# The experts' tokens gathered in 128-feature pieces and turned by VectorE, in an attention-and-experts kernel

## The chip, the core and the metric

The kernel runs on one core of a Trainium2 chip. Time is the device time of the program in microseconds (us); where several executions were timed, their median. A profile is one further execution with the profiler on; its span is the time from its first to its last instruction.

The engines: TensorE (PE in the profile; PEld is its weight loads), VectorE (DVE), ScalarE (ACT), GpSimd (POOL), which also issues the indirect DMAs, and SyncE (SP), which issues most of the others. Each engine runs its own instructions in order.

## The reference, cut to what matters

The input is x, 8 sequences of 256 tokens with 512 features. A first layer adds a gated long convolution (heads of width 8, a causal filter per head) of ctx with the normalised x to x. The second layer, in which most of the change lies, is a mixture of 16 experts; each token goes to 4 of them, each expert takes at most 256 tokens, and a shared expert works on all:

```python
scores = softmax(x @ gate_w.T); topk_w, topk_i = top_k(scores, 4)
topk_w = topk_w / (topk_w.sum(-1) + 1e-20)
# buf: the tokens of each expert by rank, at most CAP = 256; wbuf: their weights
xg = xpad[buf]
mid = silu(einsum('ech,ehi->eci', xg, w_gate)) * einsum('ech,ehi->eci', xg, w_up)
eout = einsum('eci,eih->ech', mid, w_down) * wbuf[..., None]
y = zeros.at[buf].add(eout)
shared = silu(x @ sw_gate) * (x @ sw_up) @ sw_down
```

Here x is the layer-normalised token, h runs over 512 features and i over 352 hidden units. The kernel returns x plus both.

## The kernel before, in words

All arithmetic that counts is in fp32. A tile is 128 tokens (16 of them, in the order row, then batch); 512 features are NC = 4 chunks of 128. The program order of every engine is the order of the source lines; waits come from the data only.

**Attention part** (a loop over 16 tiles n, L690). Each turn convolves two heads' worth of rows on TensorE (attend, L443, L457) with elementwise work on VectorE and GpSimd. Between these stand steps for neighbouring tiles. The new tokens of tile n-1 are normalised (xn, L745) and stored by store() (L535) to xw_d, a table in DRAM with one row per token: 512 features and 16 expert weights (ROW = 528 elements). For ten of the tiles (MILD, n = 3 to 12) the token-to-feature transpose, xnT, which the router and the shared expert use, isn't made on TensorE. ScalarE writes the normalised tile once more, with its columns permuted (xp, L749), four DMAs send it to a DRAM scratch (send_blocks, L376), one fetches it with 32-token blocks in place (fetch_blocks, L386), and VectorE transposes 32 by 32 blocks (transpose_blocks, L391, L393). The keys and queries of the next tile go the same way (kp, qp). The other tiles are transposed on TensorE (transpose_in, L126) and copied out by ScalarE. masks() (L190) makes small constant tables, in three steps in turns 6, 7 and 8.

**Shared expert.** shared_block() (L131) is a generator; fill(k) runs k steps of it wherever it stands, so that TensorE has work while others prepare. What is left runs in the loop at L921.

**Routing.** For expert e, compare(e) (L859) marks in hot which token has which slot; find(e) (L870) turns that by 16 bf16 matmuls (L875) and five small VectorE operations (L883 to L891) into idx[:, e, n], the row number for each of the 256 slots (two halves n of 128). Empty slots point to zero rows behind the tokens.

**Experts** (a loop over e, L1031; one turn is called a slot below). The order in the source is the order on each engine:
- gate_up(e): 16 matmuls with 128x256 operands for two full hidden blocks (L970; the profile counts two records for each) and the rest of 96 columns in a packed form (L982, L990); SiLU on ScalarE, products into mid on VectorE (L978, L1000, L1004)
- tokens(e+1) (L938): the gathered rows of the next expert, transposed by TensorE, 8 times 128x128 (L128), and copied out by ScalarE (L942) into xgT
- find(e+2) and gather(e+2) (L925): two indirect DMAs of GpSimd (L929), each 128 rows of 2112 bytes from xw_d, weights included
- down(e, n) for both halves: 6 matmul records each (L1012), a scaling by the slot's weight on VectorE (L1020; the weight is column 512 + e of the gathered row), and an indirect DMA of GpSimd that adds the rows to out (L1021). Each such scatter waits until the one before it has landed, since both add to the same array
- compare(e+3), and the weight loads of expert e+2 by SyncE (L816 to L821)

Gathers for experts 0 and 1 are issued ahead of the loop (L1029), and the first tokens(0) there too (L1030). The weights of the slots are written into xw_d by 16 DMAs at L915.

Chunk c holds features 128c to 128c+127, in xgT as in the rows of the weights (L816, L817: partition p of chunk c is row 128c + p).

Of the kernel before, what the change touches and what calls it, by code (L numbers as in the profile page):

```python
# [20 lines left out]
P = 128  # L21
BK = 32
# [10 lines left out]
ROW = L + E  # L33
# [19 lines left out]
def ssm_attention__then__moe_kernel(  # L53
# [34 lines left out]
    xw_d = dram.tile([T + CAP, ROW], F32, name="xw_d")  # L88
# [35 lines left out]
    def transpose_in(src):  # L124

        pt = ps_tr.tile([P, NC, P], F32, name="pt")  # L126
        for c in range(NC):
            nc.tensor.transpose(pt[:, c, :], src[:, c * P : (c + 1) * P], ident)  # L128
        return pt

# [59 lines left out]
    def masks():  # L190
# [27 lines left out]
        nc.gpsimd.tensor_copy(empty, empty_i)  # L218
        yield
# [13 lines left out]
        nc.vector.tensor_copy(tok, tok_f)  # L233
        yield
# [9 lines left out]
        masked.update(tri=tri, tri_b=tri_b, same_b=same_b, slot_f=slot_f, tok=tok, empty=empty)  # L244
        yield
# [3 lines left out]
    with ExitStack() as att:  # L249
# [284 lines left out]

        def store(n, xn):  # L535
            nc.sync.dma_start(out=by_tile(xw_d[0:T, 0:L])[n], in_=xn)
# [73 lines left out]
        for c in range(NC):  # L610
            rows = slice(c * P, (c + 1) * P)
            shared_pieces.append((swg[:, c, :], sw_gate[rows, 0 : NF * P]))
            shared_pieces.append((swu[:, c, :], sw_up[rows, 0 : NF * P]))
        rest = slice(NF * P, IS)
        by_chunk = lambda w: w[:, rest].rearrange("(c p) f -> p c f", p=P)
# [73 lines left out]
        sent_k = sent_q = sent_x = got_x = None  # L689
        for n in range(NT):  # L690
# [4 lines left out]
            tps = [toeps.pop(t * HT + hh) for hh in range(HT)]  # L695
            if more and n:
                for hh in range(HT):
                    load_blocks(seq[n + 1] * HT + hh)
            for i in range(2 if n == 0 else n + 3, min(n + 4, NT)):
                loaded[i] = load_tile(i)  # L700
            if swift and more:
                got_k, got_q = fetch_blocks(sent_k), fetch_blocks(sent_q)
# [5 lines left out]
            if n - 2 in MILD:  # L708
                transpose_blocks(xnT[:, :, n - 2, :], got_x)
# [28 lines left out]
            if n == 0:  # L738
                pg = ps_tr.tile([P, NC, P], F32, name="pg", tag="pt")
                for c in range(NC):  # L740
                    nc.tensor.transpose(pg[:, c, 0:E], gw[:, c * P : (c + 1) * P], ident[:E, :E])
                nc.scalar.copy(gwT[:, :, 0:E], pg[:, :, 0:E])
            fill(2)
            if n > 0:
                normalise(xn, xs[:, seq[n - 1], :], *xstats)  # L745
                store(seq[n - 1], xn)
                if n - 1 in MILD:
                    xp, by_block = in_blocks("xp")
                    normalise(by_block, chunked(xs[:, n - 1, :]), *xstats)  # L749
                    sent_x = send_blocks(xp)  # L750
# [14 lines left out]
            if n - 1 in MILD:  # L765
                got_x = fetch_blocks(sent_x)
            elif n > 0:
                nc.scalar.copy(xnT[:, :, seq[n - 1], :], transpose_in(xn))
                fill(1)
                ready(n - 1)  # L770
# [19 lines left out]
        nc.scalar.copy(xnT[:, :, NT - 1, :], transpose_in(xn))  # L790
# [7 lines left out]
        zeros = load.tile([P, ROW], F32, name="zeros", bufs=1)  # L798
        nc.gpsimd.memset(zeros, 0.0)
        for n in range(NSL):  # L800
            dst = slice(T + n * P, T + (n + 1) * P)
            nc.sync.dma_start(out=xw_d[dst, :], in_=zeros)
            nc.sync.dma_start(out=out[dst, :], in_=zeros[:, 0:L])
# [8 lines left out]
    def load_expert(e):  # L812
        w = wpool.tile([P, 2, NC, I], F32, name="w")
        wd = wpool.tile([P, NI, L], F32, name="wd")
        full = I // P * P
        nc.sync.dma_start(out=w[:, 0], in_=w_gate[e].rearrange("(c p) f -> p c f", p=P))  # L816
        nc.sync.dma_start(out=w[:, 1], in_=w_up[e].rearrange("(c p) f -> p c f", p=P))  # L817
        nc.sync.dma_start(
            out=wd[:, 0 : I // P, :], in_=w_down[e, 0:full, :].rearrange("(c p) f -> p c f", p=P)
        )  # L820
        nc.sync.dma_start(out=wd[0 : I - full, I // P, :], in_=w_down[e, full:, :])  # L821
        return w, wd
# [27 lines left out]
    for n in range(NSL):  # L850
        fill(1)
        nc.vector.tensor_mul(
            what[:, :, :, n, :],
            part[:, n].unsqueeze(3).broadcast_to([P, NT, E, 3]),
            tok.unsqueeze(2).broadcast_to([P, NT, E, 3]),
        )
    idx = route.tile([P, E, NSL], I32, name="idx")

# [11 lines left out]
    def find(e, hot):  # L870


        ip = ps_sm.tile([P, NSL, 3], F32, name="ip", tag="sm")
        for i in range(NT):
            nc.tensor.matmul(  # L875
                ip.rearrange("p n k -> p (n k)"),
                lhsT=hot[:, i, :],
                rhs=what[:, i, e].rearrange("p n k -> p (n k)"),
                start=(i == 0),
                stop=(i == NT - 1),  # L880
            )
        info = route.tile([P, NSL, 3], F32, name="info", bufs=2)
        nc.vector.tensor_copy(info, ip)  # L883
        who = route.tile([P, NSL], F32, name="who", bufs=2)
        gap = route.tile([P, NSL], F32, name="gap", bufs=2)
        nc.vector.scalar_tensor_tensor(
            who, info[:, :, 0], float(S), info[:, :, 1], ALU.mult, ALU.add
        )
        nc.vector.tensor_mul(gap, info[:, :, 2], empty)
        nc.vector.tensor_sub(gap, empty, gap)  # L890
        nc.vector.tensor_add(idx[:, e, :], who, gap)  # L891

# [10 lines left out]
    find(0, hots.pop(0))  # L903
    fill(2)
    nc.vector.tensor_reduce(tot, prob, AX.X, ALU.add)
# [8 lines left out]
    for n in range(NT):  # L914
        nc.sync.dma_start(out=by_tile(xw_d[0:T, L:ROW])[n], in_=prob[:, n, :])  # L915
# [3 lines left out]
    find(1, hots.pop(1))  # L919
    hots[2] = compare(2)  # L920
    while behind:  # L921
        fill(1)


    def gather(e):  # L925
        gs = []
        for n in range(NSL):
            g = ffn.tile([P, ROW], F32, name="g", bufs=6)
            nc.gpsimd.indirect_dma_start(  # L929
                out=g,  # L930
                out_offset=None,
                in_=xw_d[:, :],
                in_offset=bass.IndirectOffsetOnAxis(ap=idx[:, e, n : n + 1], axis=0),
            )
            gs.append(g)
        return gs

    def tokens(gs):  # L938

        xgT = ffn.tile([P, NC, CAP], F32, name="xgT")  # L940
        for n in range(NSL):
            nc.scalar.copy(xgT[:, :, n * P : (n + 1) * P], transpose_in(gs[n]))  # L942
# [65 lines left out]
    def down(e, n, mid, wd, g):  # L1008
# [11 lines left out]
        nc.vector.tensor_scalar_mul(o, po, g[:, L + e : L + e + 1])  # L1020
# [8 lines left out]
    gathered = {e: gather(e) for e in range(2)}  # L1029
    xgT_next = tokens(gathered[0])  # L1030
    for e in range(E):  # L1031
        w, wd = experts.pop(e)
        wt = pack(w)
        gs = gathered.pop(e)
        xgT = xgT_next
        mid = ffn.tile([P, NI, CAP], F32, name="mid")
        if e + 1 < E:
            gate_up(xgT, mid, w, wt, slice(0, CAP))
            xgT_next = tokens(gathered[e + 1])
            if e + 2 < E:  # L1040
                find(e + 2, hots.pop(e + 2))
                gathered[e + 2] = gather(e + 2)
            for n in range(NSL):
                down(e, n, mid, wd, gs[n])
            if e + 3 < E:
                hots[e + 3] = compare(e + 3)
        else:
# [3 lines left out]
            down(e, 0, mid, wd, gs[0])  # L1051
            gate_up(xgT, mid, w, wt, slice(P, CAP), range(1, NI))
            down(e, 1, mid, wd, gs[1])
# [40 lines left out]
```

## Time and profile before

| | us |
|---|---|
| median of 3 timed runs | 700.24 (698.79 to 700.52) |
| the profiled execution | 697.82 |
| its span | 696.1 |
| granted TensorE clock, mean | 0.994 |
| attention part, about | 0 to 342 |
| rest of the shared expert, with routing | 342 to 424 |
| experts 0 to 15 | 424 to 696 |

The costliest groups by line that the change touches or that stand beside it, from the profile's table of groups (busy time, mean of one):

| line, what | count | busy us | mean ns |
|---|---|---|---|
| L970 PE gate and up, 128x256 | 480 | 106.2 | 379 |
| L1012 PE down, 128x512 | 128 | 61.3 | 601 |
| L128 PE transposes of gathered rows | 128 | 16.6 | 273 |
| L942 ACT copy of them | 32 | 16.9 | 578 |
| L929 POOL gather | 32 | 32.0 | 1001 |
| L1021 POOL scatter | 32 | 51.0 | 1595 |
| L1020 DVE scaling | 32 | 24.0 | 751 |
| L393 DVE block transpose, 128x512 | 36 | 25.4 | 705 |
| L862 DVE compare | 16 | 36.5 | 2281 |

Matmuls are pipelined, and the profile models their ends, so the mean of one matmul is longer than the step from one to the next: in an expert, 32 records of L970 take 6.91 us, 0.216 each. A GpSimd indirect DMA is busy while it writes the transfer's descriptors; the bytes land later. An entry in square brackets behind a timeline line is the idle time of that engine before the instruction, and what ended it.

### The profile page before, as it was taken

To read this page: it belongs to the slowest core of one execution; us is meant where nothing else is said; L and a number is where in the kernel's file an instruction comes from. 1 tells how busy PE (TensorE), PEld (TensorE's weight loads), DVE (VectorE), ACT (ScalarE), POOL (GpSimd) and SP (SyncE) were. 2 spreads that over 40 slices of the span, in tenths; PEclk is the share of its full clock that TensorE was granted. 3 is DMA by queue.
4 is the path that set the end of the run, shared out by engine and by line. 5 is a ranking of instruction groups with operands and counts; after the bars stand their busy time and mean duration, and the time that the engine had idled before them with its cause. 6 is when DMAs were issued, how large, how long until landed. Compare 5 with 4: busy or idle time off the path is not lost.

```text
span 696.1 us, 9866 instructions
## 1 busy us (share of the span) xinstructions
PE 668.5 (96%) x3441; PEld 500.4 (72%) x3441; DVE 363.4 (52%) x834; ACT 197.7 (28%) x505; POOL 305.9 (44%) x479
## 2 busy tenths in 40 slices
PE   6889999798999999999999999999999999999994
PEld 5677886677867867867868676777777777777772
DVE  4956666778868767586456301334333444333221
ACT  3443433444342343421222001222211111221220
POOL 6667655777666676645210200222333332222321
PEclk9999999999999999999999999999999999999998
DMA  6793547646657646441037302677777777767632
GB/s 143 240 260 89 134 124 174 161 115 173 151 141 193 169 102 164 126 107 45 16 100 260 98 0 53 197 202 206 201 187 197 195 203 208 205 192 193 186 47 31
DMA packets 90930, 104.17 MB, mean 150 GB/s; under 512 B 10417, under 2 KB 63505, under 8 KB 90881
## 3 DMA queue, kind: packets, MB, share of 16 engines
q1 hardware_dynamic: 83424, 86.24, 44.3%
q0 software_dynamic: 7168, 17.04, 11.9%
q8 instruction: 27, 0.44, 0.3%
q10 hardware_dynamic: 288, 0.26, 0.2%
q14 instruction: 23, 0.18, 0.1%
HBM read 75.86 MB, written 27.66 MB: 149 GB/s over the span
## 4 chain that ended last, share of the span: by engine, by line
PE 88%; DMA 4%; DVE 4%; POOL 2%; issue 1%; ACT 1%; SPq 0%; POOLq 0%; ACTq 0%; DVEq 0%
PE sgu L157 20%; PE pgu L970 16%; PE y L457 14%; PE eo L1012 12%; PE so L174 11%; PE pgu L990 4%; PE pt L128 2%; PE pgu L982 2%; PE sgt L143 2%; PE shared L457 2%; DMA got<-sent 1%; PE ip L875 1%; PE pt L518 1%; POOL kv L434 1%; DVE y L506 1%
## 5 line engine op out<-in xcount | busy, mean ns | idle before, releaser
L457 PE MATMUL y<-kv,toep 128*128 128x288 f32 x528 | 139.9, 409 | 3.7 <-DVE f L507 2.7
L457 PEld LDWEIGHTS y<-kv,toep 128*128 128x128 f32 x528 | 99.8, 192 | 34.9 <-issue 7.6
L970 PE MATMUL pgu<-xgT,w 128*128 128x256 f32 (+1 forms) x544 | 113.8, 367 | 0.8 <-ACT xgT L942 0.8
L970 PEld LDWEIGHTS pgu<-xgT,w 128*128 128x128 f32 x544 | 98.6, 190 | 20.4 <-issue 7.7
L1021 POOL DMA_INDIRECT out<-eo_sb,idx x32 | 51.0, 1595 | 103.7 <-DMA out<-eo_sb,idx 67.8
L929 POOL DMA_INDIRECT g<-xw_d,idx x32 | 32.0, 1001 | 143.1 <-PE eo L1012 64.2
L1012 PE MATMUL eo<-wd,mid 128*128 128x512 f32 (+1 forms) x192 | 86.4, 598 | 0.0
L434 POOL TENSOR_TENSOR kv<-k 128x256 f32<-128x256 f32 x128 | 85.8, 703 | 0.0
L509 POOL TENSOR_TENSOR f<-f 128x256 f32<-128x256 f32 x60 | 43.7, 729 | 89.3 <-DVE f L507 81.5
L157 PE MATMUL sgu<-xnT,swg 128*128 128x256 f32 (+1 forms) x400 | 78.0, 338 | 0.0
L157 PE MATMUL sgu<-xnT,swu 128*128 128x256 f32 (+1 forms) x400 | 77.8, 337 | 0.0
L174 PE MATMUL so<-swd,smid 128*128 128x512 f32 x160 | 73.6, 593 | 0.0
L157 PEld LDWEIGHTS sgu<-xnT,swg 128*128 128x128 f32 x400 | 65.3, 191 | 7.4 <-issue 0.2
L157 PEld LDWEIGHTS sgu<-xnT,swu 128*128 128x128 f32 x400 | 64.6, 191 | 6.3
L1012 PEld LDWEIGHTS eo<-wd,mid 128*128 128x128 f32 (+1 forms) x192 | 35.1, 190 | 37.9 <-issue 33.6
L977 ACT ACTIVATE eact<-pgu 128x256 f32<-128x256 f32 (+1 forms) x34 | 12.7, 372 | 152.0 <-PE pgu L970 152.0
L174 PEld LDWEIGHTS so<-swd,smid 128*128 128x128 f32 x160 | 29.9, 190 | 32.4 <-issue 31.1
L978 DVE TENSOR_TENSOR mid<-eact,pgu 128x256 f32<-128x256 f32 (+1 forms) x34 | 13.8, 406 | 70.8 <-ACT eact L977 70.8
L166 ACT ACTIVATE act<-sgu 128x256 f32<-128x256 f32 (+1 forms) x50 | 17.1, 342 | 117.1 <-PE sgu L157 116.9
L480 DVE TENSOR_TENSOR y<-y,again 128x576 f32<-128x576 f32 x28 | 21.4, 766 | 53.9 <-PE y L457 37.3
L1020 DVE TENSOR_SCALAR eo_sb<-eo,g 128x512 f32<-128x512 f32 x32 | 24.0, 751 | 46.2 <-PE eo L1012 46.2
L507 DVE TENSOR_TENSOR f<-y,z 128x512 f32<-128x512 f32 x64 | 44.3, 692 | 6.6 <-DVE y L506 0.5
(171 smaller groups left out, 840.4 us busy)
## 6 DMA issues: line engine op xcount, KB each, us to landing
w<-in_L_ffn_w_gate SPq DMA_DIRECT2D x16, 704.0 KB, 4.5
w<-in_L_ffn_w_up SPq DMA_DIRECT2D x16, 704.0 KB
got<-sent SPq DMA_DIRECT2D x36, 256.0 KB, 6.1
toep<-win_d SPq DMA_DIRECT2D x28, 320.0 KB, 5.2
wd<-in_L_ffn_w_down SPq DMA_DIRECT2D x16, 512.0 KB, 4.7
xs<-in_x SPq DMA_DIRECT2D x16, 256.0 KB, 5.8
kn<-in_ctx SPq DMA_DIRECT2D x16, 256.0 KB, 6.3
xw_d<-xn SPq DMA_DIRECT2D x16, 256.0 KB, 2.9
```

The lines of the kernel that those rows point to most:

```text
L157: nc.tensor.matmul(pgu[:, k, :], lhsT=sw[:, c, f * P : (f + 1) * P], rhs=toks[:, c, :], start=(c == 0), stop=(c == NC - 1),)
L174: nc.tensor.matmul(po, lhsT=m[:, i * P : (i + 1) * P], rhs=swd[:, (f - 1) % (NF + 1), :], start=(f == 0), stop=(f == NF),)
L434: nc.gpsimd.tensor_mul(kv[:, c, 0 : ND * HB].rearrange("p (d w) -> p d w", d=ND), kh[:, c, 0:HB].unsqueeze(1).broadcast_to([P, ND, HB]), v ...
L457: nc.tensor.matmul(out, lhsT=toep[:, m * P : (m + 1) * P], rhs=rhs, start=(n == 0), stop=(n == len(pairs) - 1),)
L507: nc.vector.tensor_add(f, yd, z[:, :, :, BACK : BACK + HB])
L509: adder.tensor_add(f[:, :, 0:2, :], f[:, :, 0:2, :], f[:, :, 2:4, :])
L929: nc.gpsimd.indirect_dma_start(out=g, out_offset=None, in_=xw_d[:, :], in_offset=bass.IndirectOffsetOnAxis(ap=idx[:, e, n : n + 1], axis=0),)
L970: nc.tensor.matmul(pgu[:, k, cols], lhsT=w[:, k, c, f * P : (f + 1) * P], rhs=xgT[:, c, cols], start=(c == 0), stop=(c == NC - 1),)
L990: nc.tensor.matmul(pgu[:, 0, cols], lhsT=wt[:, c, 0:P], rhs=xgT[:, c, cols], start=(c == 0), stop=(c == NC - 1),)
L1012: nc.tensor.matmul(po, lhsT=mid[:m, f, n * P : (n + 1) * P], rhs=wd[:m, f, :], start=(f == 0), stop=(f == NI - 1),)
L1020: nc.vector.tensor_scalar_mul(o, po, g[:, L + e : L + e + 1])
L1021: nc.gpsimd.indirect_dma_start(out=out, out_offset=bass.IndirectOffsetOnAxis(ap=idx[:, e, n : n + 1], axis=0), in_=o, in_offset=None, comp ...
```

## The change

The token table is split: xn_d holds each token's 512 features as four rows of 128 (512 bytes each), pw_d the 16 weights of each token. A row of xn_d is a piece: piece i of a token holds features 128i to 128i+127, and every gather now fetches 128 pieces. Partition p of a gathered tile gets piece p // 32 of a token chosen by p % 32, so that the 32 by 32 block transposes of VectorE leave the features on the partitions: partition 32i + r holds features 128i + 4r to 128i + 4r + 3, one in each chunk. The features are thus dealt to the chunks in turn (feature 4p + c is partition p of chunk c), and gate, up, router and shared weights are loaded in that order (rows "(p c)" in place of "(c p)", so each partition of an expert's weights reads 5632 bytes in one run and not four of 1408).

What the parts become:
- store() writes xn to xn_d. For the ten MILD tiles the second normalisation (xp) and its four sends go; fetch_rows() reads the pieces straight from xn_d by four DMAs, and transpose_rows() transposes them, with a step of four elements in the source
- the TensorE transposes that remain (turn) read columns with a step of four
- find() makes two row numbers (idx for the scatter, ido for pw_d) and a bf16 table by_quart; the new rows(e) has two bf16 matmuls that spread the token numbers over the partitions, and one VectorE operation that writes idr, the piece numbers. find has eight VectorE operations in place of five
- gather(e, n): four indirect DMAs per half, each 128 pieces; gather_weights(e): two of 64-byte rows
- tokens(e): two VectorE transposes in place of eight TensorE transposes and two ScalarE copies
- in a slot the scatters are now issued after both scalings and after rows(): four gathers, a scatter, four gathers, two weight gathers, a scatter
- masks() makes three more tables (same_p, quart, mine); the weights are written to pw_d by one DMA; the rest of the shared expert runs after tokens(0) and not ahead of the first gathers; in the attention loop the key fetch comes ahead of the loads of the convolution blocks, and the query fetch ahead of the tile loads

The core of the diff:

```diff
-            if swift and more:
-                got_k, got_q = fetch_blocks(sent_k), fetch_blocks(sent_q)
...
-                if n - 1 in MILD:
-                    xp, by_block = in_blocks("xp")
-                    normalise(by_block, chunked(xs[:, n - 1, :]), *xstats)
-                    sent_x = send_blocks(xp)
...
+    def transpose_rows(dst, got):
+        nc.vector.transpose(dst, got.rearrange("p j (f c) -> p c j f", c=NC))
...
+    def rows(e, sm, by_quart):
+        ir = sm[:, 8 : 8 + NSL * NB]
+        for k in range(2):
+            nc.tensor.matmul(
+                ir,
+                lhsT=same_p[:, k],
+                rhs=by_quart[:, k].rearrange("p n j -> p (n j)"),
+                start=(k == 0),
+                stop=(k == 1),
+            )
+        nc.vector.tensor_scalar(idr[:, e, :], ir, mine[:, 1:2], None, ALU.add)
...
+    def gather(e, n, g=None):
+        if g is None:
+            g = ffn.tile([P, NSL * NB, P], F32, name="g", bufs=3)
+        for k in range(n * NB, (n + 1) * NB):
+            nc.gpsimd.indirect_dma_start(
+                out=g[:, k, :],
+                out_offset=None,
+                in_=xn_d[:, :],
+                in_offset=bass.IndirectOffsetOnAxis(ap=idr[:, e, k : k + 1], axis=0),
+            )
+        return g
...
-            nc.scalar.copy(xgT[:, :, n * P : (n + 1) * P], transpose_in(gs[n]))
+            transpose_rows(xgT[:, :, n * P : (n + 1) * P], g[:, n * NB : (n + 1) * NB, :])
...
-    gathered = {e: gather(e) for e in range(2)}
-    xgT_next = tokens(gathered[0])
+    gathered = {e: gather(e, 1, gather(e, 0)) for e in range(2)}
+    weights = {e: gather_weights(e) for e in range(2)}
+    fill(6)
+    xgT_next = tokens(gathered.pop(0))
+    while behind:
+        fill(1)
...
-            xgT_next = tokens(gathered[e + 1])
+            xgT_next = tokens(gathered.pop(e + 1))
             if e + 2 < E:
-                find(e + 2, hots.pop(e + 2))
-                gathered[e + 2] = gather(e + 2)
-            for n in range(NSL):
-                down(e, n, mid, wd, gs[n])
+                found = find(e + 2, hots.pop(e + 2))
+            outs = [down(e, n, mid, wd, wg) for n in range(NSL)]
+            if e + 2 < E:
+                rows(e + 2, *found)
+                g = gather(e + 2, 0)
+                scatter(e, 0, outs[0])
+                gathered[e + 2] = gather(e + 2, 1, g)
+                weights[e + 2] = gather_weights(e + 2)
+                scatter(e, 1, outs[1])
+            else:
+                for n in range(NSL):
+                    scatter(e, n, outs[n])
```

## The prediction, on record before the result

> **What bounds the kernel now.** I read the page's busy shares first, then the chain of waits, then the timeline of one expert, then the answers on the gathered tile and on the output.
>
> ```profile
> PE 668.5 (96%) x3441; PEld 500.4 (72%) x3441; DVE 363.4 (52%) x834; ACT 197.7 (28%) x505; POOL 305.9 (44%) x479
> ...
> PE 88%; DMA 4%; DVE 4%; POOL 2%; issue 1%; ACT 1%; SPq 0%; POOLq 0%; ACTq 0%; DVEq 0%
> ```
>
> TensorE is busy throughout and carries 88% of the chain. The experts are the part the change rewrites; the chain there repeats itself:
>
> ```profile
> 441.48 6.91 PE pgu L970 x32
> 448.39 1.02 PE pgu L982 x16
> 449.41 1.92 PE pgu L990 x8
> 452.59 5.26 PE eo L1012 x12
> 457.85 6.91 PE pgu L970 x32
> ```
>
> From one L970 to the next is 457.85 - 441.48 = 16.37 us, one slot. Gate and up take 9.86, down 5.26; the 1.25 between L990 and L1012 holds the transposes of the next expert (L128) and the index matmuls (L875). In the timeline of that slot (start, duration, engine, line) they can be seen, with what follows on VectorE and GpSimd:
>
> ```profile
> 450.96 1.01 PEld L128 LDWEIGHTS pt<-ident,g 128*128 128x128 f32 x8
> ...
> 451.94 0.56 PEld L875 LDWEIGHTS <-hot 128*128 128x128 bf16 x16
> ...
> 453.02 0.42 DVE L1004 TENSOR_TENSOR mid<-eact,pgu 64x256 f32<-64x256 f32 x1 [0.44 <-ACT eact L1003]
> ...
> 453.82 0.19 PEld L1012 LDWEIGHTS eo<-wd,mid 96*128 96x128 f32 x1 [0.24 <-DVE info L883]
> ...
> 455.09 1.02 POOL L929 DMA_INDIRECT g<-xw_d,idx  x1 [4.89 <-PE eo L1012]
> ...
> 456.42 0.98 POOL L929 DMA_INDIRECT g<-xw_d,idx  x1 [0.30 <-DMA out<-eo_sb,idx]
> ...
> 457.70 1.62 POOL L1021 DMA_INDIRECT out<-eo_sb,idx  x1 [0.30 <-issue]
> ...
> 464.50 1.58 POOL L1021 DMA_INDIRECT out<-eo_sb,idx  x1 [5.17 <-issue]
> ```
>
> GpSimd has two gathers and two scatters per slot: with the 0.30 between them a gather occupies its queue for 1.27 to 1.33 us and a scatter for 1.92, 6.4 of 16.4 us. The gathers for an expert are issued 2.6 us before the slot ends and are used 12 us into the next one: ample room.
>
> **What goes from TensorE.** Eight transposes, from weight load 450.96 to weight load 451.94: 0.98 us a slot. Not all of it is gained. The third piece of L1012 needs the last mid (L1004, ends 453.44); its weights were loaded at 453.82 and would now be wanted at 453.82 - 0.98 = 452.84, but can't be before 453.50. That is 0.66 late. The last slot but one, which has no index matmuls, shows how much of this is swallowed: its load came 0.16 later than the usual 0.43 rhythm and the loads after it were back in rhythm, so up to the usual idle of 0.24 costs nothing:
>
> ```profile
> 666.34 0.46 PEld L1012 LDWEIGHTS eo<-wd,mid 96*128 96x128 f32 x2 [0.40 <-DVE mid L1004]
> ```
>
> So 0.66 - 0.24 = 0.42 comes back as a stall. The two new bf16 matmuls of rows() cost 2 x 0.035 = 0.07 (sixteen like them take 0.56). TensorE's own slot becomes 16.37 - 0.98 + 0.42 + 0.07 = 15.9, a gain of 0.47. Ahead of expert 0 the transposes and the copy that TensorE waits for (L942) go: weight load 422.60 to 424.84, 2.2 us. The ScalarE copies (2 x 0.58 a slot) were beside TensorE; their end gains nothing more.
>
> **What GpSimd gets.** Eight gathers of 512-byte rows and two of weights (64-byte rows) in place of two. No row shows a gather of short rows. Its bounds: the gathers that are there, 0.98; below, if GpSimd's time follows the DMA packets: a scatter of single 2 KB rows takes 1.58 and the gather, whose bytes travel as two rows a packet, 0.98, that is 0.6 us for 64 packets more; short rows that share packets by eight would take (0.98 - 48 x 0.0095) = 0.52. Above, the longest gather, 1.23. I take 0.97 (1.27 with the gap): same operation, same 128 indices; the scatter's extra time has another reason at hand, since it adds and so must also read. By itself the queue then needs 10 x 1.27 + 2 x 1.92 = 16.5 us a slot: already more than TensorE's 15.9.
>
> The Trainium skill speaks for the lower end here: "DMA: Bandwidth & Descriptors", section "Anatomy of one DMA — SWDGE (gpsimd) path", lists descriptor generation as small and says that many descriptors can be emitted before their cost shows. The trace has GpSimd busy for 0.98 us with one gather, and the next waiting behind it, so I hold to the row; with generation nearly free, the change would end as in the first rival below.
>
> **The new loop, which decides.** An expert's gathers no longer stand at the slot's middle but after rows(), which on VectorE comes behind both output scalings of the slot. And VectorE, in order, now waits for the gathers itself (the transposes), ahead of find(), the scalings and rows(): so the gathers of one slot release those of the next. Once round, from the first gather:
> - four gathers, a scatter, then the start of the eighth gather: 7 x 1.27 + 1.92 = 10.8
> - its landing. For the gathers now:
>
> ```profile
> DMA to landing us min/median/max: 3.5/3.6/4.4
> ```
>
> The page's queue table gives q0 11.9% of 16 engines' 696.1 us for 17.04 MB; a gather's 0.27 MB is then 1.3 us on each engine, and a quarter of the bytes saves at most 1.0: between 2.6 and 3.6, I take 3.1 -> 13.9
> - the second VectorE transpose, 0.70 plus 0.06 to start (L393 rows, same shape; their source had stride 1, here stride 4, which no row shows; between 0.70 and twice that, I take 0.70) -> 14.7
> - find: eight small operations at the 0.16 that five take in 0.82 -> 16.0. TensorE's rows() matmuls wait for the fifth, and the next expert's gate_up stands behind them
> - two output scalings at 0.75, the index row 0.16, and 0.28 from VectorE to GpSimd as at L929 -> 17.9
>
> 17.9 us, against 16.37 now: + 1.5 a slot. Thirteen rounds lie between the gathers of expert 2 and of expert 15: 13 x 1.53 = + 20.
>
> **The tail.** Each scatter waits until the one before it has landed; without weight loads they stand 5.6 apart (668.69 and 674.27 in GpSimd's timeline). Expert 13's second scatter now comes behind ten gathers and a scatter, 10 x 1.27 + 1.92 = 14.6 after the round began, and four intervals follow: the last scatter at 37.0. Gate_up of the last expert starts at 14.8, so the last scatter comes 22.2 after it, against 687.79 - 670.04 = 17.75 now: + 4.5 (4 x 4.8 by the shortest landing, + 1; 4 x 7 by the longest, + 10).
>
> **The rest.** Ten ScalarE normalisations (0.82) and 40 sends go, 30 fetch issues come; SP and ScalarE have room there. The earlier key fetch removes waits of VectorE (9.6 us in all), but the long TensorE stall, 4.0 at 127.6, hangs on ScalarE's copy behind the query transpose (125.75), which waits for VectorE's attention work and not for a DMA. The extra masks are some 2 us of VectorE at 172 to 177, where it is full. Together between - 3 and + 2.5; I take + 0.5. The gather of the first experts starts earlier, since the 16 small writes of weights into the token table (up to 391) no longer hold it: hidden behind the shared expert. The longer weight rows (1408 to 5632 bytes) load two experts ahead, no wait there: nothing; if that cover went, they could only gain.
>
> Sum: - 2.2 - 0.5 (slot 0) + 20 + 4.5 + 0.5 = + 22.3 on the profiled execution's 697.8 (span 696.1 and 1.7 around it): 720.1. The median of the runs shown is 700.24, 2.4 above the profiled one: 722.5, forecast **722**.
>
> **Rivals.**
> 1. *Short gathers are cheap, TensorE keeps the bound* (other side). At 0.52 a gather (0.82 with gap) the loop is 17.9 - 7 x 0.45 = 14.8, under 15.9. Then 15 slots x 0.47 = - 7, - 2.2 ahead, + 0.5, tail + 0.8 (ten gathers of 0.82 hold the scatters less): - 7.9, 692. For it: the packets above. Against it: the durations 0.94 to 1.02 of all steady gathers. It decides below about 0.74 us a gather, where the whole change comes out at zero; a gather about there gives "no change", 700. Chance 0.22 for faster, 0.08 within.
> 2. *The loop doesn't close, only GpSimd's sum counts* (the second half lands in time, or VectorE isn't held): 16.5 a slot, 13 x 0.15 = + 2, with tail + 4.5, - 2.7 and + 0.5: about 704 to 707. Chance 0.10. Against it: 13.9 to land and 12.2 until VectorE asks.
> 3. *Longer gathers and landings*: at 1.23 and 4.4, the maxima of now, the loop is 17.9 + 7 x 0.26 + 1.3 = 21.0: + 60, about 762; half of that, 740. For it: four times as many DMAs on that queue. Chance 0.09 above 738.
>
> The forecast itself (711 to 738): 0.51. Faster by over 0.3% (about what a measurement tells from no change) 0.22, within 0.08, slower 0.70 = 0.51 + 0.10 + 0.09. Range: 693 to 738; below lies about half of the first rival, above the third.
>
> **What would show it.** Right: GpSimd's DMAs back to back at 1.27, the slot about 18, VectorE's second transpose waiting for the gather's DMA some 2 us a slot, TensorE idle about 2 us a slot before L970's successor, scatters of the last three experts in a row at the end. Wrong: gathers under 0.7 us; a slot of 15.9 with TensorE full; a strided VectorE transpose well over 0.7; or a changed attention part by more than 3 us.

## The result, and the profile after

The changed kernel takes 752.4 us (748.3 to 757.3, four runs) against 700.4 (698.8 to 700.7): 1.075 times as long, 95% interval 1.068 to 1.082. The forecast was 722, range 693 to 738: the direction was right, the size not. The kernels were timed in sessions: each session runs some kernels on one chip, the kernel before among them. Two further sessions gave 754.3 and 742.3 for the changed kernel; what goes with that difference is the second finding on the hardware, at the end.

The profile page of the changed kernel: the share of busy time, and two groups of its list (busy time and mean ns of one, then idle time of the engine just before, and what ended most of it).

```profile
PE 677.5 (91%) x3345; PEld 497.2 (67%) x3345; DVE 405.4 (54%) x937; ACT 172.2 (23%) x453; POOL 452.6 (61%) x608
...
L1012 POOL DMA_INDIRECT g<-xn_d,idr x128 | 147.4, 1152 | 117.5 <-DVE idr L973 65.3
...
L141 DVE STREAM_TRANSPOSE xgT<-g 128x512 f32<-128x512 f32 x32 | 34.6, 1085 | 41.9 <-DMA g<-xn_d,idr 41.9
```

TensorE fell from 96% to 91% of a longer span and no other engine is full: something goes round in a circle. GpSimd waits for VectorE's row numbers, VectorE for GpSimd's gathers. Both halves of the loop that the prediction named can be read off here.

One round, in the timeline of the third profile of the changed kernel (span 741.1; start, duration, engine, line; in brackets the idle time before and what ended it):

```profile
458.79 2.28 DVE L915 TENSOR_TENSOR hot<-pos,slot_f 128x2048 bf16<-128x2048 f32 x1
459.14 2.79 POOL L1012 DMA_INDIRECT g<-xn_d,idr  x1 [1.34 <-DVE idr L973]
462.23 0.95 POOL L1012 DMA_INDIRECT g<-xn_d,idr  x1 [0.30 <-issue]
...
471.69 0.94 POOL L1012 DMA_INDIRECT g<-xn_d,idr  x1 [0.30 <-issue]
...
474.44 1.08 DVE L141 STREAM_TRANSPOSE xgT<-g 128x512 f32<-128x512 f32 x1 [2.43 <-DMA g<-xn_d,idr]
...
475.55 0.17 DVE L937 COPY info<-ip 128x6 f32<-128x6 f32 x1
...
476.64 1.40 DVE L1113 TENSOR_SCALAR eo_sb<-eo,wg 128x512 f32<-128x512 f32 x2
477.96 0.22 DVE L973 TENSOR_SCALAR idr<-ip,mine 128x8 int32<-128x8 f32 x1
...
478.45 2.79 POOL L1012 DMA_INDIRECT g<-xn_d,idr  x1 [1.40 <-DVE idr L973]
```

From first gather to first gather 19.31 us: 12.55 to the start of the eighth gather, 2.75 until VectorE has it, 1.08 for the transpose, 1.12 for the find, 1.32 for two scalings, 0.49 to the next gather. The steady gathers are as forecast, 0.94 to 0.98 and 0.30 between. The first one is not: 2.79, and just then the compare (L915) runs on VectorE. Over the 13 rounds of this profile the mean is 19.51, with 2.91 for the landing; a slot, counted from gate_up to gate_up, is 19.46.

### The profile page after: what moved, and what is told of

It is laid out like the page before. It is cut to its first block, busy times and chain, and to the rows that moved or that the text cites. A ratio compares the mean times of both kernels' runs of the same rounds, so it can differ in the third digit from the quotient of the medians.

```text
span 746.2 us, 9834 instructions
## 1 busy us (share of the span) xinstructions
PE 677.5 (91%) x3345; PEld 497.2 (67%) x3345; DVE 405.4 (54%) x937; ACT 172.2 (23%) x453; POOL 452.6 (61%) x608
## 3 DMA queue, kind: packets, MB, share of 16 engines
q0 software_dynamic: 9728, 17.05, 12.2%
## 5 line engine op out<-in xcount | busy, mean ns | idle before, releaser
L1012 POOL DMA_INDIRECT g<-xn_d,idr x128 | 147.4, 1152 | 117.5 <-DVE idr L973 65.3
L1063 PE MATMUL pgu<-xgT,w 128*128 128x256 f32 (+1 forms) x544 | 128.9, 400 | 0.0
L1063 PEld LDWEIGHTS pgu<-xgT,w 128*128 128x128 f32 x544 | 107.7, 209 | 17.1 <-issue 1.4
L1105 PE MATMUL eo<-wd,mid 128*128 128x512 f32 (+1 forms) x192 | 90.2, 606 | 4.8 <-issue 2.6
L1117 POOL DMA_INDIRECT out<-eo_sb,idx x32 | 51.6, 1612 | 26.0 <-issue 17.9
L141 DVE STREAM_TRANSPOSE xgT<-g 128x512 f32<-128x512 f32 x32 | 34.6, 1085 | 41.9 <-DMA g<-xn_d,idr 41.9
L536 DVE TENSOR_TENSOR y<-y,q 128x512 f32<-128x512 f32 x64 | 44.8, 700 | 2.2
```

What stands on the lines that cost most here:

```text
L141: nc.vector.transpose(dst, got.rearrange("p j (f c) -> p c j f", c=NC))
L536: nc.vector.tensor_mul(yd, yd, view(qq, 0, [[qc, 2], [B, ND], [1, HB]]))
L1012: nc.gpsimd.indirect_dma_start(out=g[:, k, :], out_offset=None, in_=xn_d[:, :], in_offset=bass.IndirectOffsetOnAxis(ap=idr[:, e, k : k + 1 ...
L1063: nc.tensor.matmul(pgu[:, k, cols], lhsT=w[:, k, c, f * P : (f + 1) * P], rhs=xgT[:, c, cols], start=(c == 0), stop=(c == NC - 1),)
L1105: nc.tensor.matmul(po, lhsT=mid[:m, f, n * P : (n + 1) * P], rhs=wd[:m, f, :], start=(f == 0), stop=(f == NI - 1),)
L1117: nc.gpsimd.indirect_dma_start(out=out, out_offset=bass.IndirectOffsetOnAxis(ap=idx[:, e, n : n + 1], axis=0), in_=o, in_offset=None, comp ...
```

## The experiments

Times are medians; the ratio is to the kernel before in the same session. A slot is the mean of twelve, from gate_up to gate_up.

### First session: three parts of the loop, alone and together

Theory: the loop, lengthened by a first gather that is held while the compare reads its two operands from SBUF, and by transposes with a source step of four elements. Rival: GpSimd or DMA work by its sum.

**compare_psum**: the compare's large operand lies in PSUM.

```diff
-    nc.vector.scalar_tensor_tensor(pos, late, -float(P), pos, ALU.mult, ALU.add)
+    pos_ps = ps_tr.tile([P, NT, E], F32, name="pos_ps", tag="pt")
+    nc.vector.scalar_tensor_tensor(pos_ps, late, -float(P), pos, ALU.mult, ALU.add)
...
-            pos[:, :, e : e + 1].broadcast_to([P, NT, P]),
+            pos_ps[:, :, e : e + 1].broadcast_to([P, NT, P]),
```

> The changed kernel, but the slot positions that VectorE's compare reads lie in PSUM and not in SBUF; all else as it is. Theory (loop with a lock): the compare, an operation with two SBUF inputs that starts right behind the index row, holds up the first gather of each round, 2.79 us in place of 0.95. Then the first gather falls to about 0.95, a round from 19.95 to 18.1 us, and the whole from 752 to about 728. Rival A (the first gather is slow because it is the first after a pause or reads a fresh index row): it stays at 2.79 and the time at 752. Rival B (only the sum of GpSimd's DMAs counts): a round of 16.4, about 706.

742.2 us, ratio 1.057 (1.049 to 1.064). The timeline has the compare and the first two gathers of a round at

```profile
576.34 2.28 DVE L916 TENSOR_TENSOR hot<-pos_ps,slot_f 128x2048 bf16<-128x2048 f32 x1
576.69 0.99 POOL L1013 DMA_INDIRECT g<-xn_d,idr  x1 [4.62 <-DVE idr L974]
577.98 0.95 POOL L1013 DMA_INDIRECT g<-xn_d,idr  x1 [0.30 <-issue]
```

The compare stands beside the first gather as before and takes as long, but 2.79 became 0.99, and the eighth gather starts 10.77 us after the first, as forecast for the original loop. That the compare held the gather by its second SBUF input is shown. But the time fell by 10 us and not by 24: GpSimd now waits 4.62 for the row numbers. Of the 1.80 gained, the landing took back 0.73 (2.96 to 3.69, means of 13 rounds) and the way from the transpose to the next gather 0.59, so the round fell only from 19.95 to 19.47.

**unit_step**: the tokens are stored in permuted columns, by six more normalisations on ScalarE, so that the transpose's source has step one.

```diff
-        nc.vector.transpose(dst, got.rearrange("p j (f c) -> p c j f", c=NC))
+        nc.vector.transpose(dst, got.rearrange("p j (c f) -> p c j f", c=NC))
...
+            normalise(dealt(xp), by_feature(xs[:, n, :]), *xstats)
```

> The changed kernel, but ScalarE writes the stored tokens with their features permuted, so that VectorE's transposes read with a step of one element and not four; six more normalisations on ScalarE. Theory: the step is what made the transpose 1.085 us and not 0.70; only the second transpose of an expert lies in the loop, so a round falls by 0.38 to 19.6 and the whole by 5 to about 747. Rival (the transposes are slow because they write for TensorE or run beside GpSimd): they stay near 1.08, no change, 752. Rival B (GpSimd's sum): 0.70 but no change in time.

752.5 us, 1.074 (1.067 to 1.081): no gain. The profile's view of the transposed tile (min, median, max ns; below, VectorE's wait before it):

```profile
L141 DVE STREAM_TRANSPOSE xgT<-g x32: 666/711/714, 401.8 to 717.0; 128x512 f32<-128x512 f32 x32
...
  DMA g<-xn_d,idr: 55.5, 20
```

The step is what made the transpose 1.09 us; without it, it takes 0.71. The 12 us thus freed on VectorE came back as 13.6 us of waiting for the gathers (41.9 before).

**find_first**: find and row numbers of expert e+2 stand ahead of the transposes of e+1, so VectorE no longer waits for the gathers of the same round.

```diff
-            xgT_next = tokens(gathered.pop(e + 1))
             if e + 2 < E:
                 found = find(e + 2, hots.pop(e + 2))
-            outs = [down(e, n, mid, wd, wg) for n in range(NSL)]
+            pos_out = [down_mm(0, mid, wd)]
             if e + 2 < E:
                 rows(e + 2, *found)
+            xgT_next = tokens(gathered.pop(e + 1))
+            pos_out.append(down_mm(1, mid, wd))
+            outs = [scale(e, n, pos_out[n], wg) for n in range(NSL)]
```

> The changed kernel, but in each slot VectorE does find and the index row of expert e+2 ahead of the transposes of expert e+1, so the gathers of one slot no longer wait for those of the slot before; GpSimd's order and all sizes as they are (compare in SBUF, step of four). Theory: the loop is open, what is left is GpSimd's own sum, ten gathers at 1.25, two scatters at 1.92 and 1.84 of the compare's hold: 18.2 a slot, the whole about 729. Rival (it is not the loop but TensorE's slower clock or the landings that make the slot): near 750. Rival C (the loop alone counts and GpSimd's sum does not): TensorE's 15.9 to 16.4 a slot, about 703.

746.3 us, 1.065 (1.061 to 1.068). VectorE's wait for the gathers is gone, yet a slot is 19.7 us: the first step of the find now starts 4.2 to 4.5 us after the modelled end of the index matmuls (1.76 in all_three_again below).

**all_three**: the three edits together.

> The three edits together: positions in PSUM, step of one, find ahead of the transposes. Theory: GpSimd's ten gathers at 1.25 and two scatters at 1.92 are the bound, 16.4 a slot against 19.95, the whole about 706 (703 to 712). Rival C (GpSimd's sum does not bind): TensorE's 15.9 a slot, about 698. If the clock or landings made the slot: above 720.

763.5 us, 1.089 (1.083 to 1.094): slower than the changed kernel, where I expected 706. The theory seemed to fall. What each profile of the first session shows instead is that results of TensorE reach the others late. Here, PE and ACT in one slot of all_three (L1097 is the last gate and up piece, L1106 its activation; "remote" means that the profile finds no instruction that ended the wait):

```profile
555.98 1.99 PE L1097 MATMUL pgu<-xgT,wt 128*128 128x256 f32 x8
...
561.37 0.27 ACT L1106 ACTIVATE eact<-pgu 32x128 f32<-32x128 f32 x1 [5.92 <-remote]
...
563.50 1.24 PE L1122 MATMUL eo<-wd,mid 96*128 96x512 f32 x2 [3.32 <-DVE mid L1111]
```

The matmuls end at 557.97, ScalarE is free and starts 3.40 us later, and TensorE, which needs that result for L1122, stands still for 3.32. In the kernel before, this release takes 0.04 us in all 16 slots.

### Second session: what makes the results late?

Theories: gathers of 64-byte rows, weight pieces of 5632 bytes, or the transposes that TensorE no longer has.

**no_weights**: no weights gathers; the scale is one.

```diff
     def gather_weights(e):
+        return None
...
-        nc.vector.tensor_scalar_mul(o, po, wg[:, n, e : e + 1])
+        nc.vector.tensor_scalar_mul(o, po, ones)
```

> The weights gathers (64 bytes a row) are left out and every expert's output is multiplied by one, so the router's weights are not applied; all else is the changed kernel. It asks why TensorE's results reach ScalarE and VectorE late in the changed kernel and its three variants (0.5 to 6.9 us after the modelled end of the matmuls, against 0.04 us in the kernel before). Theory S, gathers of 64-byte rows in flight delay TensorE's signals: the first activation of the last gate and up piece starts within 0.1 us of its matmuls' end and the output scalings too, a round falls by the 0.94 us that the second scaling waited, and the time is about 738 to 741 against 752. Theory L, the experts' weights loaded in pieces of 5632 bytes do it: the lateness stays (0.5 and 2 us), 746 to 752. Theory G, the missing transposes between gate/up and the index matmuls let TensorE run dry: the lateness stays too, 746 to 752.

**small_pieces**: eight weight transfers of 1408-byte pieces.

```diff
-        nc.sync.dma_start(out=w[:, 0], in_=w_gate[e].rearrange("(p c) f -> p c f", p=P))
+        for c in range(NC):
+            nc.sync.dma_start(out=w[:, 0, c], in_=w_gate[e].rearrange("(p c) f -> c p f", p=P)[c])
```

> The experts' gate and up weights are loaded by eight transfers of 1408-byte pieces in place of two of 5632-byte pieces; nothing else differs from the changed kernel. Theory L, the large pieces delay TensorE's signals: the lateness vanishes (0.04 us), 738 to 741. Theories S and G: the lateness stays and the time is 750 to 755.

**stir_again**: eight transposes that nothing uses.

```diff
+                    for c in range(NC):
+                        nc.tensor.transpose(idle[:, c, :], w[:, 0, c, 0:P], ident)
                 found = find(e + 2, hots.pop(e + 2))
```

> Eight TensorE transposes that nothing uses are put back where the kernel before had its own, between gate/up and the index matmuls; ScalarE reads four columns of each. Theory G, TensorE runs dry there: the last mid piece is in time, the lateness and half of the half-clock windows vanish, and 14 slots gain more than the 1.04 us of the transposes costs them: 735 to 745. Theories S and L: the lateness stays, and the time is 752 to 765.

**whole_rows**: the changed kernel with whole-row gathers, TensorE transposes and the order of before.

```diff
-        for k in range(n * NB, (n + 1) * NB):
-            nc.gpsimd.indirect_dma_start(
-                out=g[:, k, :],
...
+        nc.gpsimd.indirect_dma_start(
+            out=g[:, n, :],
+            out_offset=None,
+            in_=xn_d.rearrange("(t i) f -> t (i f)", i=NB),
...
-            transpose_rows(xgT[:, :, n * P : (n + 1) * P], g[:, n * NB : (n + 1) * NB, :])
+                nc.tensor.transpose(pt[:, c, :], every(g[:, n, :], c), ident)
```

> Everything of the change but the short gathers and VectorE's transposes: each slot tile is gathered by one transfer of whole 2048-byte rows, TensorE transposes it and ScalarE copies, in the order of the kernel before; the weights' own table with its 64-byte gathers, the dealing of features to chunks with its 5632-byte pieces and the changed attention phase stay. It holds the rest of the change by itself. With TensorE's slot of 16.37 us as before, and the 2.6 us that the changed kernel gained ahead of expert 0: 697. Theories S and L: the lateness is there too (0.5 us and more), though the transposes hide some of it: 698 to 712. Theory G: no lateness, 694 to 699.

No last piece was late in any of the four (0.04 us in all 16 slots), so the second session could not tell the three theories apart: all_three_again below is on time with none of these edits. One theory falls later: best_start has no gathers of 64-byte rows, and its results were late. The other two stay open: no version of the changed kernel with small pieces or with transposes on TensorE ran in a session with late results. What the four kernels do tell:

| kernel | us | ratio (95%) | a slot | landing |
|---|---|---|---|---|
| no_weights | 737.8 | 1.054 (1.050 to 1.058) | 19.62 | 3.06 |
| small_pieces | 750.4 | 1.072 (1.068 to 1.076) | 20.20 | 3.58 |
| stir_again | 773.5 | 1.105 (1.101 to 1.109) | 22.00 | 5.45 |
| whole_rows | 698.6 | 0.998 (0.996 to 1.000) | 16.45 | |

(Landing: from the start of the eighth gather to VectorE's second transpose, mean of 13 rounds.) Each slot is 16.55 plus its landing, within 0.1: the loop holds, with on-time results too. And the landing grows with the weight loads: my transposes read the weight tile, so the load of the next gate weights went out 9.7 to 12.2 us after the round began and not 5.3 to 7.3 (third profile), into the landing of the last gathers. VectorE's wait in stir_again's timeline, where the eighth gather starts at 540.75:

```profile
540.36 0.33 SPq L864 DMA_DIRECT2D w<-in_L_ffn_w_gate  x1
...
540.75 0.95 POOL L1012 DMA_INDIRECT g<-xn_d,idr  x1 [0.31 <-issue]
...
546.77 1.08 DVE L141 STREAM_TRANSPOSE xgT<-g 128x512 f32<-128x512 f32 x1 [4.20 <-DMA g<-xn_d,idr]
```

whole_rows (698.6 against 699.8) says that the rest of the change costs nothing: expert 0 starts at 421.3 (424.8 before), a slot is 0.08 longer.

### Third session: all three edits again, and a version without the table

**all_three_again**: the same kernel as all_three.

> The same kernel as all_three, run again beside the next three. If TensorE's late results in it (3.5 us at the first activation of the last piece) belong to the kernel, they are there again and the time is 761 to 767; if they belonged to that execution or chip, they are gone and the time is 700 to 712.

699.9 us, 0.998 (0.995 to 1.000), with the same instructions in the same order on every engine. The same two lines as above:

```profile
560.07 1.99 PE L1097 MATMUL pgu<-xgT,wt 128*128 128x256 f32 x8
...
562.10 0.26 ACT L1106 ACTIVATE eact<-pgu 32x128 f32<-32x128 f32 x1 [2.56 <-PE pgu L1097]
```

Matmuls end at 562.06, ScalarE starts 0.04 later. Transfers and the instructions of the other engines last about as long in both runs; what differs is the release of TensorE's results and, behind TensorE's pauses, its clock. So the 63.6 us between the two runs of one kernel go with the late results and what follows from them. A slot is 16.33 us: GpSimd's own sum, forecast at 16.3 for this kernel. Between its DMAs GpSimd has only the 0.30 to 0.31 there, and its round is 16.39 to 16.44 throughout. The theory that had seemed to fall stands: with the loop opened, the first gather free and the step at one, GpSimd is the bound.

**all_small**: all_three with small_pieces.

> all_three with the gate and up weights loaded by eight transfers of 1408-byte pieces, the edit that took the lateness out of the changed kernel without a gain there. Theory W, late results are what made all_three slow: they are gone (0.04 us), a slot falls from 21.3 us to GpSimd's own sum (eight gathers and two weights gathers of 1.25 us, two scatters of 1.9 us: 16.3 us), 700 to 712. Theory X, the lateness is only a sign of something else, such as GpSimd's waits for the row numbers and TensorE's pauses with their half clock: a slot stays at 19 to 21 us, 740 to 765.

700.3 us, 0.998 (0.996 to 1.001), a slot 16.29. With all_three_again on time beside it, this says nothing on the pieces and late results.

**best**: all_three, and the weights come from two more columns of the index matmuls, so that GpSimd has eight gathers a slot and not ten. **best_small**: the same with small pieces.

```diff
+        nc.vector.tensor_mul(what[:, :, :, n, 3], part[:, n], prob)
+        nc.vector.tensor_sub(lgt, prob, what[:, :, :, n, 3])
+        nc.vector.tensor_mul(what[:, :, :, n, 4], part[:, n], lgt)
...
+            nc.vector.tensor_add(wts[:, e, :], info[:, :, 3], info[:, :, 4])
```

> all_three, and the slots' weights come from two more bf16 columns of the index matmuls (high and low part of the weight) in place of a table and two gathers a slot. GpSimd's sum falls to 13.8 us, so TensorE would be the bound with 16.37 - 0.98 + 0.1 = 15.5 us. If the lateness is gone as it was without the weights gathers: 15.5 to 16 us a slot, 685 to 700, faster than the kernel before. If it stays: 730 to 765.

> best with the weights loaded in 1408-byte pieces. Theory W: 685 to 700 whatever best gives. Theory X: as best, 730 to 765.

698.7 us, 0.997 (0.995 to 0.999), and 699.0, 0.997 (0.995 to 0.999). The slot is 15.92 and 15.86 us, TensorE's own, which the prediction had put at 15.9. But expert 0 starts 13 us later in best than in all_three_again (9 in best_small): TensorE waited for the new columns. In best:

```profile
385.56 0.56 PE L976 MATMUL iw<-what,hot 128*128 128x4 bf16 x16 [8.67 <-DVE what L1025]
```

### Fourth session and after: the parts once more

**after_again**, **compare_psum_again** and **find_first_again** repeat kernels; **best_start** spreads the new columns over the shared expert's pieces:

```diff
     for n in range(NSL):
+        fill(1)
         nc.vector.tensor_mul(what[:, :, :, n, 3], part[:, n], prob)
+        fill(1)
         nc.vector.tensor_sub(lgt, prob, what[:, :, :, n, 3])
...
+    fill(2)
+    weigh(hots.pop(0))
```

> The changed kernel itself, once more. The same three-edit kernel ran in 763.5 us on one chip, where TensorE's results were released up to 4 us late, and in 699.9 us on another, where they were on time (0.04 us). If the late results are of the chip and not of the kernel, the changed kernel's loop without them is 12.57 (gathers, first one held) + 2.6 to 3.5 (landing) + 1.08 + 1.1 (find) + 1.98 (two scalings, row numbers) + 0.49 = 19.8 to 20.7, hardly less than the 19.9 of its first profile: 740 to 750. If they were what made it slow, 700 to 715.

> compare_psum once more (742.2 on the chip with late results). With results on time the loop is that of the changed kernel less the 1.84 us of the held first gather: 17.9 to 18.8 a round, 716 to 728. If the late results are part of the kernel: 736 to 746.

> find_first once more (746.3 on the chip with late results, where VectorE's first step of the find waited 4.3 us longer than the matmuls took). With results on time the loop is open and the bound is GpSimd's own sum, 16.3 us, and up to 1.8 for a gather or scatter held by the compare: 16.4 to 18.1 a slot, 702 to 726. If the late results are part of the kernel: 744 to 748.

> best, whose slots of 15.9 us follow a start that came 13 us later than in all_three (435.3 against 422.2 us), because 6.8 us of VectorE's writes of the two weight columns stood ahead of the shared block's products and TensorE waited 8.7 us for them. Here those six writes alternate with pieces of the shared block, and the weight matmuls of expert 0 come two pieces later. If that wait was the cost: expert 0 starts at 422 to 425 and the time is 685 to 691. If it is not: 697 to 700.

Results were late in the fourth session too, in all four kernels: 754.3, ratio 1.073 (1.068 to 1.078); 745.7, 1.065 (1.059 to 1.070); 748.2, 1.067 (1.064 to 1.069); 720.2, 1.027 (1.024 to 1.029). What compare_psum and find_first give alone with results on time therefore stays open. In best_start expert 0 started at 425.5, so that edit worked, but ten of its 16 last pieces were released 2.2 to 2.3 us late and four 0.6, and the slots were 18.2. Two more sessions followed:

> best_start once more: expert 0 started at 425.5 us as expected, but the chip of that run released the last gate and up piece's results 2.25 us late in every slot (18.2 us a slot, 720.2 us), as two of four chips so far did in the kernels with short gathers. Where results are on time: slots of 15.9 us from a start at 423 to 426, 685 to 691. Where they are late: 718 to 724.

690.6 us, 0.985 (0.981 to 0.989), results on time, on the chip that had them late in the session before: 29.6 us less. The page of this run has TensorE back at

```profile
PE 662.5 (96%) x3361; PEld 487.6 (71%) x3361; DVE 398.0 (58%) x944; ACT 185.3 (27%) x465; POOL 397.5 (58%) x576
```

with slots of 15.91 us and expert 0 at 423.9. This version beats both kernels, the one before by 10.6 us (1.5%, four runs of one session); where results were late it lost to it.

> The changed kernel a third time; both profiles so far are from chips with late results. Where results are on time, its two neighbours (small_pieces 750.4, no_weights 737.8, both with on-time results) bound it: 738 to 750, because its loop of 19.6 to 20.2 us does not pass through the late results. If the late results were the cost after all: 700 to 725. On a chip with late results: 750 to 755.

742.3 us, 1.060 (1.055 to 1.066), results on time (0.04 us). So of the 52 us that the change cost in the recorded runs, some 42 are there without late results. The other 10 (752.4 - 742.3) go with them, but no run takes the late results away alone: the two profiled executions differ by 5.1 us in span, and the recorded runs by up to 9 among themselves.

## Why the prediction was wrong, step by step

The mechanism was the one forecast: gathers of one slot release those of the next through VectorE. Its length was not. Against the third profile, where results are on time:

| step | forecast | measured, mean of 13 |
|---|---|---|
| start of the eighth gather | 10.8 | 12.56 |
| its landing | 3.1 | 2.91 |
| second transpose | 0.76 | 1.08 |
| find | 1.3 | 1.15 |
| scalings | 1.5 | 1.32 |
| to the next gather | 0.44 | 0.49 |
| round | 17.9 | 19.51 |

- **The step that failed** is "four gathers, a scatter, then the start of the eighth gather: 7 x 1.27 + 1.92 = 10.8". All gathers were priced by rows beside which no compare ran. In the new order the compare starts 0.35 us ahead of the first gather of each round and holds it for 1.80: 23 us in thirteen rounds, while the other steps nearly cancel. compare_psum took the 1.80 away, though with late results only some 9 us of it showed in the time (754.3 and 745.7 in the fourth session); what it is worth alone with results on time isn't shown. My upper bound, the longest gather of before at 1.23, was a maximum over rows without that neighbour, so it was no bound. In the kernel before, the compare stood beside a scatter already under way, which took 1.62 (1.58 without it):

```profile
540.16 1.62 POOL L1021 DMA_INDIRECT out<-eo_sb,idx  x1 [0.90 <-DMA out<-eo_sb,idx]
540.41 2.28 DVE L862 TENSOR_TENSOR hot<-pos,slot_f 128x2048 bf16<-128x2048 f32 x1
```

- **The transpose** was taken at the lower of its two bounds, 0.70; it took 1.08, inside them. unit_step shows that the step of four is the reason.
- **Thirteen slots** of 19.46, 1.56 more than forecast, make + 20.2 us of the 22.7 by which the span of the third profile (741.1) exceeds the forecast one (696.1 + 22.3 = 718.4).
- **The tail**: the last full slot (of expert 14) and what follows it are 7.5 longer than before (1.6 and 5.9), forecast 4.5: + 3.0. The sum had no term for the 1.6: TensorE's clock was at half for 3.41 us of that slot, and its 32 records of L1063 took 8.83 us, against 7.07 for those of L970 before. The last scatter starts 22.8 after the last gate_up (forecast 22.2), and the end comes 0.9 later behind it than before. The scatters stand 5.6 to 5.7 apart (forecast 5.6), one interval 6.8:

```profile
713.76 1.59 POOL L1117 DMA_INDIRECT out<-eo_sb,idx  x1 [4.17 <-DVE mid L1071]
719.43 1.56 POOL L1117 DMA_INDIRECT out<-eo_sb,idx  x1 [4.08 <-issue]
725.07 1.56 POOL L1117 DMA_INDIRECT out<-eo_sb,idx  x1 [4.08 <-DVE mid L1097]
731.89 1.55 POOL L1117 DMA_INDIRECT out<-eo_sb,idx  x1 [5.26 <-issue]
```

- **Right**: a short gather costs what a long one does (0.95; the first rival is dead). The short rows do share packets by eight, as that rival assumed (16 packets of 4096 bytes a gather in the trace, 64 of 4224 before), but GpSimd's time doesn't follow the packets. Up to expert 0 2.0 us less (forecast 1.7), slot 0 0.7 less (0.5). TensorE's own slot of 15.9 and GpSimd's sum (16.5; 16.33 measured without the held gather) came to light as soon as the loop was opened, in best and all_three_again. One reading was loose: the gathers of before were used 9.5 us into the next slot, 12.2 after their issue; no term rests on it.
- **Half right**: the weight loads were said to cost nothing. In whole_rows they don't; but in the loop the time at which the weights load decides how long the last gathers take to land, 2.5 to 6.1 us.
- **Not foreseen**: the late results, which go with + 10 us in the recorded runs.

## What to carry to other kernels

When a change puts an instruction beside a new neighbour on another engine, price it by a row with such a neighbour, and call a maximum a bound only if its rows had one. Where an in-order engine first waits for a transfer and then computes what issues the next one, the latencies add up once a round: put the computing first (here, with the two other edits and results on time, the slot fell from 19.46 to 16.33). Time a kernel in more than one session before you believe an ablation; here one and the same kernel gave 763.5 and 699.9.

## What the runs showed of the hardware that was not expected

- **The compare holds an indirect gather.** A VectorE operation with both inputs in SBUF and 128x2048 elements (2.28 us) kept a gather at 2.79 us; with one input in PSUM the gather took 0.99. The held gather ends 0.86 us after the compare (461.93 and 461.07 above), about the time of a free one: it seems to stand still until the compare is done. The Trainium skill, "SBUF — State Buffer", section "Who interferes with whom", says that such an instruction contends with a GpSimd instruction that reads SBUF: the rows agree. The same section tells of a probe in which a two-input tensor operation didn't stall a DMA, and infers as the reason that descriptor generation needs the write interface, which such an operation leaves free; for this gather, whose row numbers lie in SBUF, the measurement says otherwise.
- **Results of TensorE can be late, by session.** The runs of one session agreed, but sessions differed: in three (the recorded runs of the changed kernel, the first and the fourth session) the changed kernel and its versions had consumers of TensorE released late, the last gate and up piece up to 1.2 us behind the modelled end of its matmuls in the changed kernel and up to 4.0 in all_three, the first step of a find in compare_psum once 6.9; in the four other sessions the last piece took 0.04 in every slot. One chip had both. The kernel before ran in 699.8 to 702.0 in every session. The instruction streams of all_three and all_three_again are the same, so they alone don't decide it; what does, and which part of the change lays a kernel open to it, stays open.
- **TensorE's clock** was granted at 0.5 for stretches of 3.41 us, ten of them during the experts in the third profile, where TensorE pauses for 1.5 to 3.1 us a round; the L1063 block of 32 records that began at 457.24, inside one of them, took 8.70 us, against 7.15 for the like block in all_three_again, which has no such stretch while TensorE works on the experts. The ten begin on a common grid of 3.41 us, and in the 3.41 us ahead of each TensorE had run no matmul for 1.68 to 3.13 us; no such step of the grid with 1.33 us or less was followed by half clock, and none lies between.
- **A VectorE transpose of 32 by 32 blocks** takes 1.08 us with a source step of four fp32 elements and 0.71 with step one, for 128x512.
